# Cross-attention and an expert FFN on one core: the read-outs and scores of a quad gathered in one cluster, and the low rank of the last quad turned between two tiles

## The chip, the core and the metric

The kernel runs on one core of a Trainium2 chip. The core has TensorE for matrix products, VectorE (DVE in the profile), ScalarE (ACT), GpSimd (POOL) and SyncE (SP), which here issues the DMAs. The engines run side by side, each through its own list of instructions in order, and wait for each other by semaphores. All data is fp32.

The metric is the device time of one execution in microseconds (us). Before the change the median of three runs is 1106.21 us (1106.09 to 1106.55).

## What is computed

There are 8 batches of 1024 rows of width 1024. Each batch has 64 memory tokens of the same width and a mask over them.

```python
# reference, cut: attention over the memory, then an expert FFN, each with a residual
h      = layernorm(x)
scores = where(mask, einsum('bsd,bmd->bsm', h, mem) / sqrt(D), -1e30)
x      = x + einsum('bsm,bmd->bsd', softmax(scores), mem)
h      = layernorm(x)
base   = h @ weight.T                         # 1024 x 1024
gates  = top 2 of softmax(h @ router_w.T) over 8 experts, made to sum to 1
Ax     = einsum('nd,erd->ner', h, lora_A)     # 8 experts of rank 16
x      = x + base + 2 * einsum('ner,ne,eor->no', Ax, gates, lora_B)
```

A batch whose mask leaves no token gets no read-out.

## The kernel before

**Tiles and quads.** The 8192 rows are 64 tiles of 128 rows. Two tiles make a pair, and two pairs make a quad: pairs u and v = u + 1. After a prologue that handles the first pairs, `quad(u)` runs for u = 2, 4, ... 30. It does the FFN of u and v, and between its matmuls the attention of later pairs: n = u + 2, m = u + 3 and f = u + 4. The whole order of every engine is written out by hand (`manual_schedule`): engines take their instructions in the order in which the Python code calls them. A `hook` is a function that is called after a given step of a product or joint, so that its work is put there.

**The FFN.** The 1024 x 1024 product is done with Strassen-like block products, which need sums of blocks. Most of these sums are on POOL. A quad consists of:
- product 1 of u, then of v, into a bank called ch (128x512, line 691);
- the low rank of each pair, `rt_low_rank_tile` (line 569), two tiles of 16 matmuls of 128x136 into pa: projections on the experts and the router's logits. ACT copies pa to axl (line 574). `rt_top` on DVE then picks two experts and scales axl (lines 582 to 603). `rt_turn_low_rank` transposes axl on TensorE into trw (line 609), ACT copies it to axwt (line 611), and `lora` (line 683) multiplies it by the experts' second factors;
- six `joint` products of u and v together, numbered 6, 2, 7, 3, 5, 4, with banks jl and ju (lines 683 and 691). Each has step hooks 0 to 7. `joint_sums` prepares its operands on POOL, and DVE adds its results to the rows (line 805).

Before pa the normalised rows go through DRAM and back in blocks (`hs`), and `rt_turn_tile` transposes them on DVE into hA and hB (line 89).

**The attention of a pair.** ACT takes sums and squares of the rows (`x_sums`, `x_squares`, lines 195 and 204). The rows are loaded a second time in blocks (`xs`, eight DMAs a pair from SP, line 83) and DVE transposes them into xT (line 89). `att_scores` multiplies xT by the turned memory memT: 32 matmuls of 128x64 weights, two side by side on the halves of the array (sct, line 410). ACT copies the scores, TensorE transposes them (sc, line 424), DVE scales and shifts them (`att_shift`), ACT takes the exponential (line 446), and DVE divides (`att_divide`, lines 454 and 455). TensorE transposes the weights (ptp, line 460), and ACT copies these to pt (line 462). `att_readout` multiplies pt by the memory: 8 matmuls with 64 rows of weights, again two side by side (ro, line 471). DVE adds the result to the rows (`att_add`). `f_sums`, `f_squares`, `f_std` and `f_rows` then normalise the rows for the FFN on ACT and DVE.

**The memory of a batch.** Four pairs share one batch. In a quad with f at the first pair of a batch (`new_mem`), `load_ms` loads the memory in blocks, `turn_mem` transposes it on DVE and sums it on POOL (lines 363 to 365), and `centre_turned` has TensorE form means (line 373) that DVE subtracts (line 374).

**Where read-out and scores stand.** Each quad has two clusters. The first follows pa of u: ro n and sct m, then trw u and ch of v. The second follows pa of v: ro m and sct f, then jl of joint 6:

```python
        if more:
            att_readout(n)
            att_scores(m)
            if u > 2:
                rt_turn_low_rank(u)
        ...
        product(v, 1, low_u)
        ...
        rt_low_rank_tile(v, 0)
        if more:
            att_turn_p(m)
        rt_low_rank_tile(v, 1, (lambda: centre_turned(b)) if new_mem else None)
        ...
            att_readout(m)
        if far:
            att_scores(f)
```

**Buffers.** There are eight PSUM banks: six in ps_pp (`bank_of`: ch, ro, jl, ju, means), one in ps_at (sct, sc, ptp) and one in ps_rt (pa, trw). A ring of five SBUF tiles serves xs, xT, the rows h and hs, and ms.

Of the kernel before, what the change touches and what calls it, by code (L numbers as in the profile page):

```python
# [10 lines left out]
F32 = mybir.dt.float32  # L11
# [13 lines left out]
def kernel(  # L25
# [61 lines left out]
    def transpose_blocked(dst, src):  # L87

        nc.vector.transpose(  # L89
            dst.rearrange("p k (t i) -> p t k i", i=NB),  # L90
            src.rearrange("p t (k i) -> p t k i", i=NB),
        )

    xts, xss, mems = {}, {}, {}

    def load_xs(u: int):

        xss[u] = []
        for r in range(2):
            xs = ring.tile([P, 4, QD], F32, tag="ring", name=f"xs_{u}_{r}")  # L100
            load_blocked(xs, xf[(2 * u + r) * P : (2 * u + r + 1) * P, :])
            xss[u].append(xs)

    def load_xt(u: int):
        xts[u] = []
# [237 lines left out]
    def load_ms(b: int):  # L343

        msr = ring.tile([P, D], F32, tag="ring", name=f"ms_{b}")
        n = M // NB * QD
        ms = msr[:, :n].rearrange("p (t c) -> p t c", c=QD)
        load_blocked(ms, mem[b])
        ones = msr[:, n : n + P]
        nc.gpsimd.memset(ones, 1.0 / D)  # L350
        mcs[b] = ms, ones, msr[:, n + P : n + P + M], msr

    def turn_mem(b: int):

        mt = memp.tile([P, KD, M], F32, tag="memT", name=f"memT_{b}_True", bufs=1)
        ms, ones, of_k, msr = mcs[b]
        transpose_blocked(mt, ms)
        if b == 1:
            nc.vector.tensor_reduce(of_k, mt.rearrange("p k m -> p m k"), AX.X, ALU.add)
        else:  # L360
            by = nc.gpsimd.tensor_tensor
            s4 = msr[:, : 4 * M].rearrange("p (k m) -> p k m", m=M)
            by(s4, mt[:, :4], mt[:, 4:], ALU.add)
            by(s4[:, :2], s4[:, :2], s4[:, 2:], ALU.add)
            by(of_k, s4[:, 0], s4[:, 1], ALU.add)
        mem_ts[b, True] = mt

    def centre_turned(b: int):

        _, ones, of_k, _ = mcs.pop(b)  # L370
        mt = mem_ts[b, True]
        means = bank_of(f"means_{b}")[:, :M]
        mm(means, ones, of_k, start=True, stop=True)
        tt(mt, mt, means.unsqueeze(1).to_broadcast([P, KD, M]), ALU.subtract)
# [16 lines left out]
    def xT_tile(u: int, r: int):  # L391
        t = ring.tile([P, KD, P], F32, tag="ring", name=f"xT_{u}_{r}")
        x_ts.setdefault(u, []).append(t)
        return t

    def att_turn_pe(u: int, r: int, later: bool = False):
        t = xT_tile(u, r)
        return transpose_pe((t[:, :KH, :], t[:, KH:, :]), xts[u][r], f"x{u}_{r}", later)

    def att_turn(u: int):  # L400
        for r in range(2):
            transpose_blocked(xT_tile(u, r), xss[u][r])

    def att_scores(u: int):

        mt = mem_ts[u // PPB, u > 1]
        sct = ps_at.tile([2 * M, P], F32, tag="at", name=f"sct_{u}")
        for k in range(KD):
            for r in range(2):
                mm(  # L410
                    sct[r * M : (r + 1) * M, :], mt[:, k, :], x_ts[u][r][:, k, :],
                    start=(k == 0), stop=(k == KD - 1),
                )
        scs[u] = small.tile([2 * M, P], F32, tag="tp", name=f"scts_{u}", bufs=2)
        nc.scalar.copy(scs[u], sct)
# [39 lines left out]
        tt(s, s, rden.unsqueeze(2).to_broadcast([P, 2, M]), ALU.mult)  # L455
        ps[u] = s

    def att_turn_p(u: int):
        ptp = ps_at.tile([2 * M, P], F32, tag="at", name=f"ptp_{u}")
        nc.tensor.transpose(ptp, ps.pop(u).rearrange("p j m -> p (j m)"), ident)  # L460
        pts[u] = small.tile([2 * M, P], F32, tag="tp", name=f"pt_{u}", bufs=2)
        nc.scalar.copy(pts[u], ptp)

    def att_readout(u: int):
# [13 lines left out]
    def att_add(u: int):  # L478
        for r in range(2):
            att_add_tile(u, r)  # L480
# [121 lines left out]
            ax_e = axl[:, r, :ER].rearrange("p (e r) -> p e r", r=R)  # L602
            tt(ax_e, ax_e, we[:, r, :].unsqueeze(2).to_broadcast([P, E, R]), ALU.mult)

    def rt_turn_low_rank(u: int):
        axl = axls.pop(u)
        trw = ps_rt.tile([ER, 2, P], F32, tag="rt", name=f"trw_{u}")
        for r in range(2):
            nc.tensor.transpose(trw[:, r, :], axl[:, r, :ER], ident)  # L609
        axwts[u] = small.tile([ER, 2, P], F32, tag="axwt", name=f"axwt_{u}", bufs=2)  # L610
        nc.scalar.copy(axwts[u], trw)
# [66 lines left out]
    def add(u: int, bank, r: int, c: int):  # L678
        xc = xts[u][r][:, ts(c, HB)]
        tt(xc, bank, xc, ALU.add)  # L680
# [39 lines left out]
            for to in {1: ((0, 0),), 6: ((0, 1),), 7: ((1, 0),), 8: ((1, 1),)}[i]:  # L720
                add(u, chain, *to)

    def one_add(u: int):

        for to in ((0, 0), (0, 1), (1, 0)):
            add(u, pps[u][1], *to)

    def t_of(u: int):

# [43 lines left out]
        by(s3, up[:, :HK], lo[:, :HK], ALU.subtract)  # L773
        jss[i] = s1, s2, s3, s4

    def joint(i: int, u: int, hooks, final: bool = False):

# [13 lines left out]
        def to_x(p, src, first: int, n: int):  # L793
            if i == 6:
                t = t_of(p)[:, first : first + n]
                if n == HH and (p == u and first == 0 or v == NP - 1):
                    nc.scalar.copy(t, src)
                elif n == HH:
                    nc.vector.tensor_copy(t, src)
                else:  # L800
                    tt(t, src, t, ALU.add)  # L801
                return
            for row, col in BOTH.get(i, ((r, c),)):
                xc = xts[p][row][:, col * HB + first : col * HB + first + n]
                tt(xc, src, xc, ALU.add)  # L805
# [273 lines left out]

    def quad(u: int):  # L1080

        v, n, m, f = [u + i for i in range(1, 5)]
        more = n < NP
        far = f < NP
        b = f // PPB
        new_mem = far and f % PPB == 0

        product(u, 1, (lambda: att_sc(n)) if u == 2 else None, 1)
        if more and u > 2:
            x_sums(m)  # L1090
        if new_mem:
            mask_bias(b)
        pending.pop()()
        if u == 2:
            att_divide(n)
        one_add(u)
        rt_low_rank_tile(u, 0)
        if u == 2:
            att_turn_p(n)
        rt_low_rank_tile(u, 1)  # L1100
        if u == 2:
            att_turn(m)
        rt_turn_tile(v, 0)
        rt_top(u)
        rt_turn_tile(v, 1)
        rt_sum_3(u)
        rt_sums(v)
        if more and u > 2:
            x_squares(m)
        if new_mem:  # L1110
            load_ms(b)
        if far:
            load_xs(f)
            load_xt(f)
        if more:
            att_readout(n)
            att_scores(m)
            if u > 2:
                rt_turn_low_rank(u)
                x_root(m)  # L1120
                att_add(n)

        low_u = {3: lambda: rt_turn_low_rank(u)}
        if more:
            low_u = {0: lambda: att_sc(m), 2: lambda: product(u, 8)}
            if u == 2:
                low_u[1] = lambda: rt_turn_low_rank(u)
        product(v, 1, low_u)
        if more:
            att_rstd(m)  # L1130
            att_exp(m)
            if u == 2:
                att_add(n)
                att_divide(m)
        else:
            product(u, 8)
        product_add(u, 8)
        if more:
            f_sums(n)
            if u > 2:  # L1140
                att_divide(m)
        if new_mem:
            turn_mem(b)
        one_add(v)
        rt_low_rank_tile(v, 0)
        if more:
            att_turn_p(m)
        rt_low_rank_tile(v, 1, (lambda: centre_turned(b)) if new_mem else None)
        joint_sums(6, u)
        rt_sum_3(v)  # L1150
        if far:
            att_turn(f)
        rt_top(v)
        if more:
            f_squares(n)
            f_std(n)
            att_readout(m)
        if far:
            att_scores(f)
        if new_mem:  # L1160
            load_mem(b)
        if more:
            att_add(m)

        hooks = {7: [lambda: rt_turn_low_rank(v)]}
        if more:
            row_0, row_1 = f_rows_steps(n)
            hooks = {2: [row_0], 5: [lambda: rt_turn_low_rank(v), row_1]}
        end_6 = joint(6, u, hooks)
        joint_sums(2, u)  # L1170

        def low_v():
# [5 lines left out]
            for p in (u, v):  # L1178
                six_add(p)

        hooks = {1: [six]}
        if far:
            x_stats(f)
            hooks[3] = [lambda: att_sc(f)]
        if new_mem:
            void_mem(b)
        if (f + 2) % PPB == 0 and f + 2 < NP:
# [19 lines left out]
            hooks[5].append(lambda: att_exp(f))  # L1207
        end_3 = joint(3, u, hooks)
        joint_sums(5, u)
        if m + 2 < NP:  # L1210
            load_xs(m + 2)

        hooks = {1: [end_3]}
        if far:
# [8 lines left out]
        def rows_0():  # L1223
            end_5()
            for p in (u, v):
                store(p, 0)
                if not more:
                    store(p, 1, ts(1, HB))
            if m + 2 < NP:
                load_xt(m + 2)  # L1230

        hooks = {1: [rows_0]}
        if more:
            hooks[3] = [lambda: rt_sums(n)]
        if m + 2 < NP:
            hooks[5] = [lambda: att_turn(m + 2)]
        end_4 = joint(4, u, hooks, not more)

        def last():
# [56 lines left out]
```

## Time and profile before

| what | value |
|---|---|
| median of 3 runs | 1106.21 us |
| the profiled execution | 1106.56 us |
| its span, first to last instruction | 1104.7 us |
| instructions | 17542 |
| DMA traffic | 174.01 MB, mean 158 GB/s |
| ch (line 691), 248 matmuls 128x512 from hA | 115.8 us busy |
| pa (line 569), 1024 matmuls of 128x136 | 71.1 + 69.9 us busy |
| ro (line 471), 256 matmuls with 64 weight rows | 63.6 us busy |
| sct (line 410), 960 matmuls with 64 weight columns | 62.0 us busy |
| trw (line 609), 64 transposes | 13.3 us busy |
| sums of a tile on ACT (lines 195 and 204), mean of one | 1.05 and 1.15 us |
| xT transposes on DVE (line 89), mean of one | 1.23 us |
| xs loads (line 83), from issue to landing | 3.6 us |

The profile is one execution with the hardware's profiler on. Lines are those of the kernel before. "Busy" counts an instruction from its start to its end; matmuls overlap each other in TensorE's pipeline, so that a mean duration is longer than the distance from one start to the next. In a timeline each row gives the start, the duration of the run of equal instructions that begins there, the engine, the line and operation, out and in by the program's names, the shapes and how many there are. A bracket tells how long the engine was idle before and what released it. The 1.86 us between the span and the time of the profiled execution lie outside the program's instructions.

### The profile page before, as it was taken

Reading aid. Unit: us, or ns where it says so; the run is one execution under the profiler, and the core shown is the slowest. Engines: PE = TensorE matmul, PEld = TensorE weight load, DVE = VectorE, ACT = ScalarE, POOL = GpSimd, SP = SyncE. Lnnn points to the kernel's source line nnn. Section 1 sums busy time; section 2 is a strip of 40 time slices with the busy share of each in tenths; the row PEclk is TensorE's granted clock in tenths of the full one; section 3 lists DMA queues with packets and bytes.
Section 4 is the critical chain, followed back from the end, with each engine's and each line's share of the span. In section 5 each row is a group of like instructions: output and inputs, shape, how many; then the busy total and the mean of one; then the engine's idle time right before and its main releaser. Section 6 shows DMA issues by size and latency. Waiting matters only on the chain.

```text
span 1104.7 us, 17542 instructions
## 1 busy us (share of the span) xinstructions
PE 1095.7 (99%) x5864; PEld 848.1 (77%) x5864; DVE 810.8 (73%) x2063; ACT 555.3 (50%) x1063; POOL 575.9 (52%) x647
## 2 busy tenths in 40 slices
PE   8999999999999999999999999999999999999998
PEld 6554787887878778787887878778787887878877
DVE  6666968777786768867678686777868787686665
ACT  4577554718357282663727547173562826545010
POOL 0079564735637265473635647266372744637382
PEclk9999999999999999999999999999999999999999
DMA  9857356374554735456265553754446453532301
GB/s 230 210 177 222 113 166 201 100 238 132 154 182 136 222 109 183 151 164 218 77 211 162 154 190 101 215 166 157 153 139 203 145 190 132 158 131 91 138 1 77
DMA packets 104922, 174.01 MB, mean 158 GB/s; under 512 B 12929, under 2 KB 77441, under 8 KB 104833
## 3 DMA queue, kind: packets, MB, share of 16 engines
q1 hardware_dynamic: 104832, 172.90, 50.3%
q8 instruction: 47, 0.77, 0.3%
q14 instruction: 43, 0.34, 0.1%
HBM read 107.84 MB, written 65.01 MB: 156 GB/s over the span
## 4 chain that ended last, share of the span: by engine, by line
PE 98%; DVE 1%; ACT 0%; DMA 0%; issue 0%; SPq 0%; DVEq 0%; ACTq 0%
PE jl L691 28%; PE ju L691 21%; PE pa L569 11%; PE ch L691 10%; PE sct L410 6%; PE ro L471 5%; PE ju L683 4%; PE jl L683 3%; PE plain L691 3%; PE ch L683 2%; PE j L691 1%; PE trw L609 1%; DMA xt<-in_x_dram 0%; PE tr_x L385 0%; PE b L691 0%; PE ptp L460 0%
## 5 line engine op out<-in xcount | busy, mean ns | idle before, releaser
L805 DVE TENSOR_TENSOR xt<-jl,xt 128x256 f32<-128x256 f32 x421 | 191.3, 484 | 115.8 <-PE jl L691 75.6
L805 DVE TENSOR_TENSOR xt<-ju,xt 128x256 f32<-128x256 f32 (+1 forms) x210 | 110.6, 550 | 69.9 <-PE ju L691 67.3
L623 POOL TENSOR_TENSOR s<-hA,hB 128x512 f32<-128x512 f32 x31 | 39.6, 1278 | 208.8 <-PE jl L691 92.8
L195 ACT ACTIVATE junk<-xt 128x1024 uint8<-128x1024 f32 x60 | 63.2, 1053 | 138.2 <-DMA xt<-in_x_dram 137.7
L735 POOL TENSOR_TENSOR xt<-xt,hA 128x512 f32<-128x512 f32 x90 | 111.3, 1275 | 23.5 <-DVE hA L801 23.4
L691 PE MATMUL ch<-w,hA 128*128 128x512 f32 x248 | 115.8, 593 | 0.0
L630 POOL TENSOR_TENSOR hA<-hA 128x512 f32<-128x512 f32 x31 | 39.4, 1272 | 141.3 <-PE pa L569 141.3
L691 PE MATMUL ju<-w,s_j 128*128 128x256 f32 x360 | 94.3, 384 | 0.2
L691 PE MATMUL ju<-t,s_j 128*128 128x256 f32 x360 | 92.5, 379 | 0.0
L680 DVE TENSOR_TENSOR xt<-ch,xt 128x512 f32<-128x512 f32 x124 | 79.4, 680 | 8.4 <-PE ch L691 4.5
L680 DVE TENSOR_TENSOR xt<-ro,xt 128x512 f32<-128x512 f32 x128 | 79.2, 676 | 3.3 <-PE ro L471 3.3
L691 PEld LDWEIGHTS ju<-t,s_j 128*128 128x128 f32 x360 | 66.2, 190 | 16.3 <-issue 3.6
L691 PEld LDWEIGHTS ch<-w,hA 128*128 128x128 f32 x248 | 44.6, 190 | 42.7 <-issue 41.8
L691 PEld LDWEIGHTS ju<-w,s_j 128*128 128x128 f32 x360 | 63.9, 190 | 16.4 <-issue 7.4
L691 PE MATMUL jl<-t,s 128*128 128x256 f32 x300 | 76.0, 384 | 0.0
L569 PEld LDWEIGHTS pa<-art_sb,hA 128*128 128x128 f32 x512 | 66.3, 190 | 9.0 <-issue 5.0
L89 DVE STREAM_TRANSPOSE xT<-xs 128x1024 f32<-128x1024 f32 x60 | 72.6, 1228 | 0.5
L410 PEld LDWEIGHTS sct<-xT,memT_True 128*64 128x64 f32 x960 | 53.1, 137 | 24.8 <-issue 12.1
L569 PE MATMUL pa<-art_sb,hB 128*128 128x136 f32 x512 | 71.1, 280 | 0.0
L569 PE MATMUL pa<-art_sb,hA 128*128 128x136 f32 x512 | 69.9, 279 | 0.0
L204 ACT ACTIVATE junk<-xt,of_x 128x1024 uint8<-128x1024 f32 x60 | 68.7, 1145 | 1.5
L253 ACT ACTIVATE junk<-xt,of_f 128x1024 uint8<-128x1024 f32 x60 | 68.7, 1145 | 1.5
(205 smaller groups left out, 2448.6 us busy)
## 6 DMA issues: line engine op xcount, KB each, us to landing
xt<-in_x_dram SPq DMA_DIRECT2D x64, 512.0 KB, 4.6
out_dram<-xt SPq DMA_DIRECT2D x62, 512.0 KB, 2.7
xs<-in_x_dram SPq DMA_DIRECT2D x240, 128.0 KB, 3.6
hd<-h SPq DMA_DIRECT2D x60, 512.0 KB, 2.7
hs<-hd SPq DMA_DIRECT2D x240, 128.0 KB, 3.2
mem<-in_ctx_dram SPq DMA_DIRECT2D x16, 256.0 KB, 3.8
w<-in_w_t_dram SPq DMA_DIRECT2D x16, 256.0 KB, 10.2
ms<-in_ctx_dram SPq DMA_DIRECT2D x28, 64.0 KB, 2.5
```

What stands on the lines that cost most here:

```text
L89: nc.vector.transpose(dst.rearrange("p k (t i) -> p t k i", i=NB), src.rearrange("p t (k i) -> p t k i", i=NB),)
L195: nc.scalar.activation(nowhere, xts[u][r], AF.Identity, accum_out=sm[:, r, :])
L204: nc.scalar.activation(nowhere, xts[u][r], AF.Square, bias=nm[:, r, :], accum_out=ss[:, r, :],)
L253: nc.scalar.activation(nowhere, xts[u][r], AF.Square, bias=nm[:, r, :], accum_out=ss[:, r, :])
L410: mm(sct[r * M : (r + 1) * M, :], mt[:, k, :], x_ts[u][r][:, k, :], start=(k == 0), stop=(k == KD - 1),)
L471: mm(ro, pts[u][rows, :], m[rows, ts(c, HB)], start=True, stop=True)
L569: mm(pa[:, r, :], h, art_sb[:, k, :], start=(k == 0), stop=(k == KD - 1))
L680: tt(xc, bank, xc, ALU.add)
L683: mm(bank, axwts[u][:, r, :], lb_sb[:, c0 : c0 + n], start=alone, stop=True, skip_group_check=True)
L691: mm(bank, a[:, k, :], w[:, k, :], start=(start and k == 0), stop=(k == n - 1), skip_group_check=True)
L735: nc.gpsimd.tensor_tensor(xc, xc, t_of(u), ALU.add)
L805: tt(xc, src, xc, ALU.add)
```

## The change

The diff moves the attention one pair further ahead, with a new name g = u + 5.

- **One cluster.** In the quads u = 4 to 26 both clusters are replaced by one behind pa of v: ro n, sct f, sct g, ro m, then jl of joint 6. The scores of m are already there from the quad before; `att_scores(g, True)` writes to a bank of ps_pp, and `sc m` is transposed in ch of v. All four transposes xT of f and g stand ahead of the cluster on DVE. The quad u = 2 has two clusters (ro n, sct m and sct f, sct g, ro m), u = 28 has ro n between the tiles of pa v, and ro m ahead of joint 6.
- **The low rank of u.** trw u moves from the cluster to between the two tiles of pa v, with a bank of its own from ps_pp. In the last quad, u = 30, it moves there from behind ch of v, and `product(u, 8)` (the low rank into ch u) follows pa of v.
- **Loads.** `load_xs` takes single tiles. In joint 4 SP issues, behind the stores of the first tiles, both tiles of xt g, both xs of f + 2 and the first of g + 2; the second xs of g and xt f come early in the next quad.
- **Memory.** load_ms, turn_mem and centre_turned of the next batch move to the quad before the one with its first pair f: behind sct g, in joint 6 (hook 5) and in joint 2 (hook 5). The sums are one `tensor_reduce` on DVE in place of three additions on POOL.
- **Smaller moves.** x_squares m follows x_sums m directly, both ahead of pa u's copy on ACT. `one_add(v)` is split, its last part in joint 6. `f_squares`, `f_std` and `f_rows` of n go to joints 6 and 2. pt m is written over s m.

```diff
     def turn_mem(b: int):
...
-        if b == 1:
-            nc.vector.tensor_reduce(of_k, mt.rearrange("p k m -> p m k"), AX.X, ALU.add)
-        else:
-            by = nc.gpsimd.tensor_tensor
-            s4 = msr[:, : 4 * M].rearrange("p (k m) -> p k m", m=M)
-            by(s4, mt[:, :4], mt[:, 4:], ALU.add)
-            by(s4[:, :2], s4[:, :2], s4[:, 2:], ALU.add)
-            by(of_k, s4[:, 0], s4[:, 1], ALU.add)
+        nc.vector.tensor_reduce(of_k, mt.rearrange("p k m -> p m k"), AX.X, ALU.add)
...
-    def att_scores(u: int):
+    def att_scores(u: int, apart: bool = False):
...
+        if apart:
+            sct = bank_of(f"sct_{u}")[:, :P]
+        else:
+            sct = ps_at.tile([2 * M, P], F32, tag="at", name=f"sct_{u}")
...
     def quad(u: int):
...
-        if more and u > 2:
+        if late:
             x_sums(m)
+            x_squares(m)
...
         rt_turn_tile(v, 0)
         rt_top(u)
+        if late:
+            x_root(m)
+            product(v, 1, lambda: att_sc(m))
+            att_rstd(m)
+            att_shift(m)
+            att_exp(m)
         rt_turn_tile(v, 1)
+        if late and far:
+            att_turn_tile(f, 0)
+            load_xs(g, (1,))
         rt_sum_3(u)
         rt_sums(v)
...
+        if late:
+            att_divide(m)
+            if far:
+                att_turn_tile(f, 1)
+            rt_low_rank_tile(v, 0)
+            rt_turn_low_rank(u, bank_of(f"trw_{u}")[:, : 2 * P])
+            one_add(v, (0,))
...
         else:
+            product(v, 1)
+            rt_low_rank_tile(v, 0)
+            rt_turn_low_rank(u, bank_of(f"trw_{u}")[:, : 2 * P])
+        if far:
+            for r in range(2):
+                att_turn_tile(g, r)
+        if late and not far:
+            att_readout(n)
+            att_add(n)
+        rt_low_rank_tile(v, 1)
+        if late:
+            att_turn_p(m, True)
+        if not early:
             product(u, 8)
-        product_add(u, 8)
...
         joint_sums(6, u)
         rt_sum_3(v)
+        if late and far:
+            att_readout(n)
+        product_add(u, 8)
+        if late and far:
+            att_add(n)
         if far:
             att_scores(f)
+            att_scores(g, True)
...
+        if far or not more:
+            rt_top(v)
+        if more:
+            att_readout(m)
...
         hooks = {1: [six]}
         if far:
             x_stats(f)
             hooks[3] = [lambda: att_sc(f)]
+        if more:
+            hooks[3].append(lambda: f_rows(n))
+        if next_mem:
+            hooks[5].append(lambda: centre_turned((f + 2) // PPB))
...
-            if m + 2 < NP:
-                load_xt(m + 2)
+            if far:
+                load_xt(g)
+            if f + 2 < NP:
+                load_xs(f + 2)
+                load_xs(g + 2, (0,))
```

## The prediction

> **What bounds the kernel now.** I read the shares first, then the chain of waits, because a busy share alone does not say what sets the end.
>
> ```profile
> PE 1095.7 (99%) x5864; PEld 848.1 (77%) x5864; DVE 810.8 (73%) x2063; ACT 555.3 (50%) x1063; POOL 575.9 (52%) x647
> ...
> PE 98%; DVE 1%; ACT 0%; DMA 0%; issue 0%; SPq 0%; DVEq 0%; ACTq 0%
> ```
>
> TensorE is busy 99% and carries 98% of the chain; the clock row is 9s throughout. So time is saved only where TensorE issues fewer matmuls or issues the same ones more densely. The change keeps the matmuls, so I look for density: start-to-start steps in TensorE's timeline, taken from undisturbed stretches and from both clusters of a quad.
>
> ```profile
> 514.59 1.09 PE L569 MATMUL pa<-art_sb,hB 128*128 128x136 f32 x8
> 515.61 1.99 PE L471 MATMUL ro<-mem,pt 64*128 64x512 f32 x8
> 517.53 1.97 PE L410 MATMUL sct<-xT,memT_True 128*64 128x128 f32 x32
> 519.42 0.44 PE L609 MATMUL trw<-ident,axl 128*128 128x128 f32 x2
> 519.70 1.02 PE L691 MATMUL ch<-w,hA 128*128 128x512 f32 x2
> ...
> 524.11 1.09 PE L569 MATMUL pa<-art_sb,hA 128*128 128x136 f32 x8
> 525.03 1.09 PE L569 MATMUL pa<-art_sb,hB 128*128 128x136 f32 x8
> ...
> 529.93 1.97 PE L410 MATMUL sct<-xT,memT_True 128*64 128x128 f32 x32
> 531.83 1.99 PE L691 MATMUL jl<-t,s 128*128 128x256 f32 x8
> ...
> 596.72 2.42 PE L410 MATMUL sct<-xT,memT_True 128*64 128x128 f32 x32
> 599.07 1.99 PE L691 MATMUL jl<-t,s 128*128 128x256 f32 x8
> ```
>
> The first number is the start. Eight pa take 525.03 - 524.11 = 0.92, a step of 0.116. A pair of ro steps 0.429 (as every 128x512 does), a pair of sct 0.109, a trw 0.109. So from 514.59 to 519.70 dense issue would need 8 x 0.116 + 4 x 0.429 + 16 x 0.109 + 2 x 0.109 = 4.61 us; it took 5.11. The **0.50** too much sits where the tile shape changes (128x128, 64x128, 128x64), in single starts: pa to ro 0.197 over, ro to sct 0.147, sct to trw 0.156. The second cluster (to jl) loses 0.548, its last step being 0.204. Both: 1.047 per quad. The last two pairs show a second loss: sct to jl is 1.90 in one quad and 2.35 in the next. That is 0.456 in each of the six quads that begin a new batch of memory, and there the row of the waits and DVE's timeline name it:
>
> ```profile
> PEld sct L410 <- DVE xT L89: 8.1, 15, 0.8
> ```
> ```profile
> 594.16 0.69 DVE L374 TENSOR_TENSOR memT_True<-memT_True,means 128x512 f32<-128x512 f32 x1 [0.55 <-PE means L373]
> 594.76 2.36 DVE L89 STREAM_TRANSPOSE xT<-xs 128x1024 f32<-128x1024 f32 x2
> ```
>
> The scores start at 596.72 while DVE is still turning their second tile (to 597.1), because turning and centring the memory (memT, means) stood ahead.
>
> **The twelve quads u = 4 to 26.** *Switches.* One cluster ro n, sct f, sct g, ro m has four changes: pa to ro 0.197, ro to sct 0.147, sct to ro, ro to jl 0.202 (a cluster of ro alone loses 0.399 in all, less 0.197). Sct to ro is not in the trace: at least 0.147 (ro to sct), at most 0.204 (sct to full); I take 0.20, since both ends leave the sct shape for a 64- or 128-row one. Sum 0.746, gain 0.30 x 12 = **3.6** (0.05 x 12 more at the low end).
>
> *New memory.* In six quads turn_mem and centre_turned leave the cluster's approach for joints 6 and 2 of the quad before, and the sums go from POOL to DVE. DVE's xT then no longer waits for them: 6 x 0.456 = **2.74**. After these clusters the first jl steps lose a further 0.06 to 0.075, which should go too: 6 x 0.07 = 0.4. In the joints DVE has room: about 0.7 for the transpose (128x512), an estimated 0.7 for the reduce (same 512 columns), 0.69 for the centring, once in two quads, where it idles 0.27 of the time.
>
> *The order that must hold.* With t = 0 at the first ch of u and the steps above, TensorE runs pa u 3.87 to 7.57, ch v from 7.57, sc m 8.43, pa v tile 0 at 11.11, trw u 12.97, tile 1 13.19, ptp m 15.04, ch u's low rank 15.15, ro n 16.10, sct f 18.02, sct g 19.82, ro m 21.67, jl of joint 6 23.59. What each wait finds, with durations of before's rows in the new order:
> - trw u (12.97) needs rt_top of u, which ends 10.76 on DVE. It now sits in a bank of its own, so that pa and trw do not exchange one. The ch low rank behind it (15.15) waits for ACT's axwt copy, 0.37 after 13.2: covered by 1.5.
> - ptp m (15.04) needs the divided s. DVE: shift and reduce to 11.72, both transposes of v's second tile to 13.01, xT f 0 to 14.09, reciprocal, divide at 14.29, done 14.5. Cover 0.45. Behind a late ptp stand both ch's low rank and the cluster.
> - sct g waits for its xs. These four DMAs wait on SP for the slot that hB v 1 leaves (13.01); four such loads landed 4.15 to 4.2 us after their first issue (582.29 to 586.49), so 17.2, just when xT g 1 can start (17.42). It ends 18.6; cover 1.2. Sct g also takes the bank of ch u, read by product_add to 19.23 (cover 0.5).
> - jl and ju of joint 6 want banks that the ro n adds (done 21.5) and the first ro m add (24.7) free: cover 0.65 at ju (25.42).
> - ptp and pt in place save nothing and cost nothing: one ACT copy either way. The split one_add and the later f_rows are beside PE; joint 2's low rank wants axwt v, cover 0.45.
>
> *ACT and SP.* x_sums m and x_squares m (1.17 and 1.26 a tile) now both precede ACT's axl copy (7.77), so the second xt m must land by 3.87 (0.45 late costs nothing yet). Before it was there by 2.05 to 3.23, in two quads at 4.2. In joint 4 six xs transfers (0.43 to 0.48 issue each on SP) now queue directly behind it, in place of loads that came later; below nothing is excluded, since the xt itself is issued no earlier. Between 0 and 0.5 late; I take 0.3, which passes the tolerance in few quads: **-0.4** in all.
>
> **The three other quads.** u = 28 keeps two clusters, both of ro alone (before 0.50 with sct, and 0.40). The first moves between pa's tiles; about 0.15 of switches goes, but its sct is now done in the quad before and joint 6 comes too early for DVE and ACT: a new wait, estimated 0.45 from the same rows laid in order. **-0.3**. u = 2 keeps two clusters, with one change of shape more (0.2) and sct 7 waiting about 0.55 for its xs; the 0.57 by which its second cluster exceeds 0.55 goes: **-0.2**. In the last quad:
>
> ```profile
> 1052.92 1.12 PE L683 MATMUL ch<-lb_sb,axwt 128*128 128x512 f32 x2 [0.46 <-ACT axwt L611]
> ```
> ```profile
> 1060.27 1.30 POOL L630 TENSOR_TENSOR hA<-hA 128x512 f32<-128x512 f32 x1
> ```
> ```profile
> 1061.60 0.37 ACT L797 COPY hA<-ju 128x256 f32<-128x256 f32 x1 [1.65 <-POOL hA L630]
> 1062.02 1.13 PE L691 MATMUL ju<-t,s_j 128*128 128x256 f32 x4
> ```
>
> Trw and the wait for axwt (0.154 + 0.655) go behind pa. But POOL's chain does not move: hA is released at 1061.57, ACT copies, and the matmul at 1062.02 is already 0.10 late for it. So the 0.81 is given back there. Only later, where trw of v at 1063.86 waited 0.256 and its neighbour 0.056 for DVE's rt_top, is **+0.3** left, because that starts earlier.
>
> **Sum.** 3.6 + 2.74 + 0.4 - 0.4 - 0.3 - 0.2 + 0.3 = 6.2. The profiled execution took 1106.56 (span 1104.7 and 1.86 around it): 1100.4. The median shown, 1106.21, is 0.35 lower; I say **1100.2**.
>
> **A rule against the change.** The new place of the divide is under POOL's rt_sums of v. A 128x128 divide with both inputs in SBUF is in the trace on both sides:
>
> ```profile
> 524.00 0.73 POOL L770 TENSOR_TENSOR s_j<-s 128x256 f32<-128x256 f32 x1
> ```
> ```profile
> 524.37 0.50 DVE L455 TENSOR_TENSOR s<-s,of_s 128x128 f32<-128x128 f32 x1
> ...
> 590.92 0.29 DVE L455 TENSOR_TENSOR s<-s,of_s 128x128 f32<-128x128 f32 x1
> ```
>
> Under POOL it ended only after POOL's end (524.73), 0.21 longer than with POOL idle. The Trainium skill (SBUF — State Buffer, Who interferes with whom) makes it a rule: a DVE instruction with two SBUF inputs contends with a GpSimd one that reads SBUF, and the loser is blocked for the whole instruction. Here POOL's instructions are not 0.73 but 1.27 us. By the 0.21 row ptp keeps 0.25 of cover. By the rule it depends on which one: POOL's first sum runs 13.09 to 14.36, the next from 14.44. A divide at 14.29 slips into the gap and ends 14.5; one more than 0.15 later is blocked to 15.71. I take the gap, as both sides count from the same event, the end of hB v 1.
>
> **Rivals.**
> - *The gap is missed* (slower). s ends 15.85, ptp waits 0.81, in 12 quads 9.7: about **1110**. For it: 0.15 of room. Against: the spacings on both engines repeat.
> - *The second xt is late by 1 us or more.* axl u, rt_top u and the low rank behind it slide, about 0.55 x 12 = 6.6, which eats the gain: **1106.6**. For it: two quads at 4.2 already. Against: SP's order keeps xt ahead of the xs.
> - *A part fails*: xs g lands 1.5 late, so that sct g waits 0.3 x 12, or switching shapes costs as much in one cluster as in two and only the memory's stalls go: **1103.5**.
>
> **Chances.** Forecast 0.56 (alone 1098.6 to 1102.4), a part failing 0.13, xt late 0.14, gap missed 0.17. A change under 0.2% (2.2 us) can't be told from none here: faster is below 1104.0, slower above 1108.4. So faster 0.69, same 0.14, slower 0.17. The range 1098.6 to 1107.0 leaves out the gap missed and little more.
>
> **What would show it.** Right: in the quads pa to jl with about 0.75 over dense steps, ptp at its step behind pa, quads of new memory as long as the others, the ju at the last quad's joint 6 waiting near 0.9. Wrong: an idle before ptp with a divide over 1 us; axl copies later than 0.2 after pa; sct g preceded by a wait on xT or on ch.

## The result and the profile after

The changed kernel took **1108.33 us** (median of 20 runs, 1105.28 to 1112.11), the kernel before 1106.12 (20 runs, 1105.73 to 1106.86). The ratio is 1.002, with a 95% interval of 1.0012 to 1.0028. So it is slower by about 2 us where 6 us less were forecast, and what is new besides is the spread: 6.8 us between runs, where it was 1.1. The profiled execution is one of the long ones: 1111.43, 3.1 above the median, with a span of 1109.7.

The page of the kernel after, parts 1 and 4:

```profile
PE 1092.1 (98%) x5864; PEld 846.1 (76%) x5864; DVE 815.8 (74%) x2069; ACT 557.3 (50%) x1063; POOL 567.1 (51%) x629
...
PE 80%; DMA 8%; DVE 6%; ACT 3%; SPq 1%; issue 1%; POOL 1%; DVEq 0%; ACTq 0%
```

TensorE is busy 3.6 us less in a span 5.0 us longer, and the chain that ended last, 98% TensorE before, now runs through DMA for 8% and through DVE and ACT for 9%. Some quads wait for transfers. First a quad that doesn't, TensorE's timeline (the first number is the start):

```profile
190.55 1.02 PE L691 MATMUL ch<-lb_sb,axwt 128*128 128x512 f32 x2
191.51 1.99 PE L476 MATMUL ro<-mem,pt 64*128 64x512 f32 x8
193.42 3.71 PE L411 MATMUL sct<-xT,memT_True 128*64 128x128 f32 x64
197.07 1.99 PE L476 MATMUL ro<-mem,s 64*128 64x512 f32 x8
198.99 1.35 PE L699 MATMUL jl<-t,s 128*128 128x256 f32 x5
```

This is the one cluster. From the last ch ahead of it to the second jl it loses 0.75 us over the dense steps of the prediction, which was the sum forecast (0.746). From the first sct to the second ro it takes 197.07 - 193.42 = 3.65 for 32 pairs, of which the change from sct to ro is 0.20 over the dense step. Such a quad is 66.26 us long from ch to ch, or 66.48 where means are formed in it; before it was 66.56, or 67.31 with new memory. Twelve quads without a wait are 796.2, against 803.2 before: 7.0 gained. But they took 806.4 in this execution, because of two kinds of wait, 10.1 us in all. The first is ahead of the second tile of pa v. In the quad that begins at 578.90:

```profile
591.88 0.38 PE L617 MATMUL trw<-ident,axl 128*128 128x128 f32 x2
593.34 1.19 PE L574 MATMUL pa<-art_sb,hA 128*128 128x136 f32 x8 [1.08 <-DVE hA L89]
...
595.52 0.30 PE L462 MATMUL ptp<-ident,s 128*128 128x128 f32 x1
```

Two trw need 0.22; here the next start is 1.46 later. DVE's hA v 1 was late, since rt_top u ahead of it waited for axl. DVE's timeline shows that wait, and ACT's what was behind it:

```profile
589.06 0.24 DVE L587 MAX8 top<-axl 128x8 f32<-128x8 f32 x2 [2.40 <-ACT axl L579]
```
```profile
584.83 1.06 ACT L194 ACTIVATE junk<-xt 128x1024 uint8<-128x1024 f32 x1 [4.25 <-DMA xt<-in_x_dram]
...
586.24 1.15 ACT L203 ACTIVATE junk<-xt,of_x 128x1024 uint8<-128x1024 f32 x1
...
587.52 1.15 ACT L203 ACTIVATE junk<-xt,of_x 128x1024 uint8<-128x1024 f32 x1
588.66 0.36 ACT L579 COPY axl<-pa 128x272 f32<-128x272 f32 x1
```

The second xt of m lands at 584.74, 5.84 after the quad's start. One sum and two squares later ACT copies axl, 9.76 after the start and not 7.77, as in a quad without a wait. Six quads lose 6.85 us in this way. The rows of SP's issues show what stands behind that xt (SP's timeline, then the DMA view of a window that holds the second xt's issue alone: KB each, us from issue to landing):

```profile
575.88 1.48 SPq L107 DMA_DIRECT2D xt<-in_x_dram  x2
577.48 9.59 SPq L83 DMA_DIRECT2D xs<-in_x_dram  x12
587.17 0.85 SPq L874 DMA_DIRECT2D out_dram<-xt  x2
```
```profile
xt<-in_x_dram SPq DMA_DIRECT2D x1, 512.0 KB, 7.7
```

The second wait is inside the cluster (TensorE, then DVE, in the quad that begins at 308.30):

```profile
326.32 1.97 PE L411 MATMUL sct<-xT,memT_True 128*64 128x128 f32 x32
329.82 1.97 PE L411 MATMUL sct<-xT,memT_True 128*64 128x128 f32 x32 [1.53 <-DVE xt L688]
```
```profile
327.95 1.25 DVE L89 STREAM_TRANSPOSE xT<-xs 128x1024 f32<-128x1024 f32 x1 [1.99 <-DMA xs<-in_x_dram]
329.12 0.65 DVE L688 TENSOR_TENSOR xt<-ch,xt 128x512 f32<-128x512 f32 x1
```

DVE waits 1.99 for the second xs of g, and product_add of ch u, whose bank sct g takes, is queued behind that transpose. The releaser named for sct g is this add; the cause is the DMA one step further back. Four quads lose 3.3 us here. Both figures belong to this long execution. In one of median length the two waits together cost about 7 us and not 10.1 (an estimate: 10.1 less the 3.1 between the two, if nothing else differs).

### The profile page after: what moved, and what is told of

Same layout as the page of the kernel before. It is cut to its first block, busy times and chain, and to the rows that moved or that the text cites. A ratio compares the mean times of both kernels' runs of the same rounds, so it can differ in the third digit from the quotient of the medians.

```text
span 1109.7 us, 17564 instructions
## 1 busy us (share of the span) xinstructions
PE 1092.1 (98%) x5864; PEld 846.1 (76%) x5864; DVE 815.8 (74%) x2069; ACT 557.3 (50%) x1063; POOL 567.1 (51%) x629
## 4 chain that ended last, share of the span: by engine, by line
PE 80%; DMA 8%; DVE 6%; ACT 3%; SPq 1%; issue 1%; POOL 1%; DVEq 0%; ACTq 0%
PE jl L699 26%; PE ju L699 20%; PE pa L574 6%; PE ro L476 5%; PE ch L699 5%; PE sct L411 5%; DMA xt<-in_x_dram 4%; PE ju L691 3%; PE jl L691 3%; PE plain L699 3%; PE ch L691 2%; DMA out_dram<-xt 2%; DVE xt L814 2%; ACT junk L203 2%; DMA xs<-in_x_dram 1%; PE j L699 1%
## 5 line engine op out<-in xcount | busy, mean ns | idle before, releaser
L295 ACT ACTIVATE h<-xt,of_f 128x1024 f32<-128x1024 f32 x60 | 71.2, 1232 | 23.1 <-DVE of_f L291 17.2
```

Source lines behind the costliest of these rows:

```text
L295: nc.scalar.activation(h, xts[u][r], AF.Identity, bias=nmr[:, r, :], scale=rstd[:, r, :])
```

## The experiments

Each ratio is to the kernel before, run beside it on the same chip. Its medians there were 1106.66 (beside the xs behind the stores, the four left there, the xt of f ahead, and both edits), 1106.25 (beside the two with loads from ACT and the last quad) and 1106.38 (beside the whole rows and ACT's order). What is said of single quads is read from one profiled execution of each.

**The xs loads behind the stores.** In place of right behind xt m in joint 4:

```diff
             if far:
                 load_xt(g)
-            if f + 2 < NP:
-                load_xs(f + 2)
-                load_xs(g + 2, (0,))
...
         def last():
             end_4()
             if more:
                 for p in (u, v):
                     store(p, 1)
+            if f + 2 < NP:
+                load_xs(f + 2)
+                load_xs(g + 2, (0,))
```

> The changed kernel, but in each quad the twelve xs loads that SP issues behind the second xt of m go behind the last two stores of the quad instead (some 4 us later). Theory A (the second xt shares the DMA engines with the xs loads issued right behind it and lands late): the second xt lands by 4.2 us after the quad's start in every quad, as before the change, in place of up to 5.9; ACT copies axl at 7.77; no wait stands between trw u and the second tile of pa v (six waits of 0.27 to 1.25 us in the profile of the changed kernel); about 4 to 5 us come off the median, 1103.5 to 1104.5, and the runs spread less. The waits before sct g (3.3 us) stay. Theory B (it is the sum of the traffic, or DRAM, that is slower, whatever the order): the second xt lands as late as now and the time stays at 1107.5 to 1109. Theory C (the xs are now late in turn): a wait of xT f on the xs before the cluster, 1106 or more.

Measured: **1103.14** (6 runs, 1101.88 to 1104.69), ratio 0.9968 [0.9956, 0.998]. The second xt of m lands between 2.24 and 3.27 in all twelve quads, axl is copied at 7.77 in each, and no wait is left at pa v. Before sct g two waits are left (1.31 and 0.70). That these fell too, from 3.3 to 2.0, was not expected, and the median is a little below the range. SP's order (the sixteen are the twelve and then the second xs of g) and the landing of that xt in this kernel:

```profile
572.55 1.47 SPq L107 DMA_DIRECT2D xt<-in_x_dram  x2
576.82 3.88 SPq L874 DMA_DIRECT2D out_dram<-xt  x2
580.80 9.55 SPq L83 DMA_DIRECT2D xs<-in_x_dram  x16
```
```profile
xt<-in_x_dram SPq DMA_DIRECT2D x1, 512.0 KB, 4.9
```

These are the same bytes in another order: theory A holds. B is refuted by the landing, C by the absence of a wait of xT f.

**Four of the twelve left there.**

```diff
             if f + 2 < NP:
-                load_xs(f + 2)
-                load_xs(g + 2, (0,))
+                load_xs(f + 2, (0,))
...
+            if f + 2 < NP:
+                load_xs(f + 2, (1,))
+                load_xs(g + 2, (0,))
```

> As the first of these runs, but four of the twelve xs loads (512 KB) stay right behind the second xt of m. Theory A: the delay grows with what is issued behind: the second xt lands between, up to about 5.0 us after the quad's start, few or no waits at pa v, 1103.5 to 1106. Theory B: as the changed kernel, 1107.5 to 1109.

Measured: 1105.76 (13 runs, 1103.24 to 1108.35), ratio 0.9996 [0.9988, 1.0004]. The second xt lands between 2.10 and 5.01. With part of the loads behind it part of the delay is there, and the spread comes back with it (5.1 us between runs, 2.8 with none left there).

**The same bytes as whole rows.** With True, `load_xs` issues one DMA of 512 KB for a tile in place of four. For these three tiles this kernel leaves out the blocking that the scores need; the work of every engine stays.

```diff
-                load_xs(f + 2)
-                load_xs(g + 2, (0,))
+                load_xs(f + 2, (0, 1), True)
+                load_xs(g + 2, (0,), True)
```

> The changed kernel, but the three xs tiles that SP loads right behind the second xt of m in joint 4 are loaded as whole rows (three DMAs of 512 KB with rows of 4 KB, in place of twelve of 128 KB with pieces of 1 KB): the same bytes in the same place, all issued within 1.5 us. The blocks of these tiles are then not those that the scores need, so the attention's output is not the reference's. If it is the bytes behind it that make the second xt late, its landing is as late as now, up to 5.9 us after the quad's start, and the waits at pa v stay: 1106 to 1110. If it is the short pieces, the second xt lands by 4.2 us in every quad, the waits at pa v go: 1102 to 1104.5.

Measured: 1104.12 (7 runs, 1102.51 to 1105.74), ratio 0.9979 [0.9967, 0.999]. The second xt lands by 3.67 in ten quads, and at 4.57 and 4.64 in two. Most of the delay goes with the short pieces (or the number of DMAs, which changes with them); in two quads a part remains with the bytes alone. Neither theory holds by itself.

**Both xt of f ahead of the second xs of g.**

```diff
             att_turn_tile(f, 0)
+            load_xt(f)
             load_xs(g, (1,))
...
-        elif far:
-            load_xt(f)
```

> The changed kernel, but SP issues both xt of f ahead of the four loads of the second xs of g, not behind them. If xs g lands late because the xt are behind it in the queue, then its last DMA lands within 3 us of its issue in every quad (now up to 4.8), the waits before sct g (3.3 us over four quads in the profile) go, and the waits at pa v stay: 1105 to 1107. If the four DMAs are late because they wait for the slot of hB v 1 alone, nothing changes: 1107.5 to 1109. If the xt, now in flight ahead, delay xs g more: above 1109.

Measured: **1132.4** (5 runs), ratio 1.0232 [1.0218, 1.0246]: a miss in size, but the third outcome. These xt wait on SP for a slot that the last stores leave, and then go out about 2 us ahead of the xs. In one quad (SP's timeline, and the DMA view of the four xs):

```profile
533.40 1.55 SPq L107 DMA_DIRECT2D xt<-in_x_dram  x2
535.82 1.75 SPq L83 DMA_DIRECT2D xs<-in_x_dram  x4
```
```profile
xs<-in_x_dram SPq DMA_DIRECT2D x4, 128.0 KB, 4.3
```

With two xt in flight ahead of them, the xs take 4.3 us in this quad, and 5.0 (median) in all twelve against 2.6 in the changed kernel. Every quad now waits before sct g. The second xt of m comes past 4.3 in eleven quads and not six; no run shows why.

**Both edits.**

> The changed kernel with both edits of SP's order. If both waits come from transfers queued behind, neither is left in the twelve quads, each of which takes 66.25 us, or 66.48 with means: 796.4 for the twelve, and with what the other quads take in the profile of the changed kernel 1101.5 in all, range 1100.5 to 1103, spread as small as before the change. If the order only moves the collision, 1105 or more.

Measured: **1151.96** (5 runs, 1149.12 to 1156.98), ratio 1.041 [1.0391, 1.0429]. The order only moved the collision, and worse than thought. With the xs later, both xt of f queue behind twelve xs and still ahead of the second xs of g. DVE's row of waits, and sct g on TensorE in one quad:

```profile
DVE xT L89 <- DMA xs<-in_x_dram: 46.4, 12, 5.4
```
```profile
552.95 3.36 PE L411 MATMUL sct<-xT,memT_True 128*64 128x128 f32 x32 [3.89 <-DVE xt L688]
556.24 1.99 PE L476 MATMUL ro<-mem,s 64*128 64x512 f32 x8
```

A long wait can cost twice. From this sct g to ro it is 556.24 - 552.95 = 3.29 us, where a quad without a wait has 1.85: the granted clock from 552.37 to 556.50 was 0.59. The waits before sct g are 38.2 of the 56.1 us that the twelve quads lose, and the mean granted clock of this execution is 0.985 (1.0 with the first edit alone), which is some 17 of its 1155 us (an estimate: 0.015 of them).

**The xt of f from ACT, late.** ACT issues them behind its copy of sct f, when the second xs of g has landed. With the first edit, and alone:

```diff
             att_scores(f)
+            if late:
+                load_xt(f, nc.scalar)
             att_scores(g, True)
```

> The kernel with the xs loads behind the stores, and in addition the two xt of f are issued by ACT behind its copy of sct f (some 20 us after the quad's start) and not by SP right behind the second xs of g. If the two waits before sct g that were left there (1.31 and 0.70 us) come from the xt right behind, they go, the twelve quads take 66.25 or 66.48 us each, and the median is 1101.0 to 1102.0, spread within 1 us. If they come from something else, or ACT's issue holds up its copies, 1103 or more.

Measured: **1102.09** (5 runs, 1101.94 to 1102.44), ratio 0.9963 [0.995, 0.9977]. The chain is TensorE's again, the spread is gone, and in eleven of the twelve quads the steps run on without a wait:

```profile
PE 93%; DVE 2%; DMA 2%; SPq 1%; POOL 1%; issue 0%; ACT 0%; DVEq 0%; ACTq 0%
```
```profile
587.22 0.38 PE L617 MATMUL trw<-ident,axl 128*128 128x128 f32 x2
587.44 1.09 PE L574 MATMUL pa<-art_sb,hA 128*128 128x136 f32 x8
...
589.29 0.27 PE L462 MATMUL ptp<-ident,s 128*128 128x128 f32 x1
...
592.28 3.71 PE L411 MATMUL sct<-xT,memT_True 128*64 128x128 f32 x64
```

One wait of 0.40 before sct g is left, in the quad u = 8, and the median is just above the range expected. This version is faster than both kernels.

> The changed kernel with this second edit alone: the xs loads stay right behind the second xt of m, the xt of f are issued by ACT. Theory A (two separate collisions): the waits before sct g go, those at pa v stay: 1105.5 to 1107.5, with a spread of several us. If the late xt of m alone makes the quads late and xs g only follows it, no change: 1107.5 to 1109.

Measured: 1104.23 (10 runs, 1102.13 to 1108.63), ratio 0.9985 [0.9975, 0.9996]: better than expected. Two waits before sct g (0.97 and 0.69) and, in five quads, waits of up to 0.9 at pa v and ptp remain in its profile; the second xt of m lands past 4.3 in five quads, at 5.15 at the latest. That the waits at pa v shrink too, from 6.85 to about 1.9, was not foreseen, and its cause stays open. So the two collisions are not separate: in these profiles each edit by itself lessens both waits.

**ACT's order.** Is it the late xt, or that x_squares m now stands ahead of the axl copy?

```diff
             x_sums(m)
-            x_squares(m)
...
+            x_squares(m)
             x_root(m)
```

> The changed kernel, but ACT takes x_squares m behind its copy of axl u and the exponential of rt_top, not ahead of the copy. The order on ACT is then no longer what makes a late xt m count: axl is copied at 7.77 even where the xt lands at 5.9. But the root, and with it s m, comes 2.5 us of squares later: DVE waits for it ahead of hA v 1, so that pa v's second tile waits about 1.4 us and ptp a little more in every quad: 15 to 25 us in all, 1118 to 1126. If ACT has the room, the waits at pa v go and the time is 1103 to 1105.

Measured: 1130.36 (one run). ACT in one quad, and TensorE there:

```profile
594.93 0.39 ACT L579 COPY axl<-pa 128x272 f32<-128x272 f32 x1 [1.01 <-PE pa L574]
```
```profile
601.80 1.19 PE L574 MATMUL pa<-art_sb,hA 128*128 128x136 f32 x8 [1.29 <-DVE hA L89]
```

axl is on time in all twelve quads, though the xt lands at up to 5.46. But each quad pays 1.46 at pa v and 0.36 behind it, 21.8 in all, and u = 28 another 4.4, which was not in the expectation. So the two conditions are tied: the squares must come early for s m, and then the xt must be early for axl.

**The last quad as before**, on the kernel with the xs behind the stores:

```diff
-            product(v, 1)
-            rt_low_rank_tile(v, 0)
-            rt_turn_low_rank(u, bank_of(f"trw_{u}")[:, : 2 * P])
+            product(v, 1, {3: lambda: rt_turn_low_rank(u)})
+            product(u, 8)
+            product_add(u, 8)
+            rt_low_rank_tile(v, 0)
```

> The kernel with the xs loads behind the stores, and in the last quad the low rank back at its old place: trw u behind ch v, then ch u's low rank, then pa v. If the 0.81 us is given back at joint 6 as predicted, the wait there falls from 1.06 to about 0.1 to 0.3 us, and from the last quad's first ch to the end it takes 0.2 to 0.4 us more than with the change (63.6 us). If the turn itself was worth its 0.81, it takes 0.8 more.

Measured (one run): from the last quad's first ch to the end of the span 63.96, against 63.52 with the change in the kernel it was made from. The rows of this run, and of the changed kernel:

```profile
1048.99 1.12 PE L691 MATMUL ch<-lb_sb,axwt 128*128 128x512 f32 x2 [0.46 <-ACT axwt L619]
...
1057.12 1.03 PE L699 MATMUL jl<-t,s_j 128*128 128x256 f32 x4
1058.09 1.13 PE L699 MATMUL ju<-t,s_j 128*128 128x256 f32 x4
```
```profile
1065.37 1.03 PE L699 MATMUL jl<-t,s_j 128*128 128x256 f32 x4
1067.30 1.13 PE L699 MATMUL ju<-t,s_j 128*128 128x256 f32 x4 [0.90 <-ACT hA L806]
```

With the change the wait for axwt goes, and the one at joint 6 (jl to ju, over four steps of 0.216) grows from 0.11 to 1.06. Of the 0.81, 0.30 (the changed kernel against the one before) to 0.44 (this pair) is kept.

## Why the prediction was wrong

As printed, its terms add to 6.14 and not 6.2, and 6.2 below the median of 1106.21 is 1100.0 and not 1100.2; neither slip matters. Term by term, by the profiles:

- **Switches, new memory and the jl behind it** (6.7): right. Twelve quads without a wait gain 7.0, the cluster loses 0.75 as worked out, and sct to ro costs 0.20, as taken.
- **The second xt of m** (-0.4): the step that failed. "Between 0 and 0.5 late; I take 0.3, which passes the tolerance in few quads." It was up to 1.7 later than its latest landing before (5.84 against 4.13), passed the tolerance of about 4.3 in six quads, and cost 6.85 us. The mechanism was named, and the rival was given one chance in seven. That its price, 6.6, is close to 6.85 is luck: 6.6 was twelve quads at 0.55, and the 6.85 are six quads at 0.62 to 1.61. The reason set against it, that SP's order keeps the xt ahead of the xs, was no reason: the xt did land ahead of them in every quad, but late.
- **The second xs of g**: "cover 1.2" was computed from four loads that had landed 4.15 to 4.2 after their first issue. Now, with two xt issued behind them, the last landed up to 6.1 after it, and they cost 3.3 us. These two terms, 10.1 together in this execution, turn the gain of 7.0 into a loss. They were held as separate rivals and never added, so the range ended at 1107.0.
- **The gap for the divide**: right. In the quad that begins at 308.30 POOL's first sum ends at 322.93 and the next starts at 323.01:

```profile
321.65 1.27 POOL L631 TENSOR_TENSOR s<-hA,hB 128x512 f32<-128x512 f32 x1 [5.19 <-DVE hB L89]
323.01 1.28 POOL L632 TENSOR_TENSOR s<-s,hA 128x512 f32<-128x512 f32 x1
```
```profile
322.78 0.30 DVE L456 TENSOR_TENSOR s<-s,of_s 128x128 f32<-128x128 f32 x1
```

  The divide starts under the first sum and ends at 323.08. In all twelve quads it takes 0.29 or 0.30, as long as with POOL idle, and ends 0.14 to 0.15 behind the sum, as it did before the change (524.87 behind 524.73). Whether the sum held it up for its first half, as the rule cited has it, these rows can't tell. The slower case on record did not occur; ptp is late only in quads where hA v 1 already was.
- **u = 28** (-0.3): mis-sized. One sct (1.74) left this quad, yet it is only 0.39 shorter. So 1.35 was given back, where 0.3 was forecast (a new wait of 0.45 less 0.15 of switches). It was given back at joint 6, where jl and ju wait for ACT and DVE:

```profile
1006.29 1.10 PE L699 MATMUL jl<-t,s_j 128*128 128x256 f32 x4 [0.68 <-ACT hA L806]
...
1008.11 1.13 PE L699 MATMUL ju<-t,s_j 128*128 128x256 f32 x4 [0.49 <-DVE hA L808]
```

- **u = 2** (-0.2): -0.8, mis-sized too. The ch of u = 4 starts 2.53 later; 1.74 of it is that sct, now done here, the rest the wait for xT g 1 (0.59), the extra switch and the means. **u = 30** (+0.3): +0.30.

Without the two waits the sum of the measured terms is 7.0 - 0.8 - 1.35 + 0.30 = 5.15, which makes 1101.4 of the profiled 1106.56; the version with both loads out of the way took 1102.09 (median). The forecast was a good account of TensorE's steps and a bad one of the DMA queue.

## What to carry to other kernels

When a change packs an engine more densely, write down for each transfer when it must have landed, and judge it by what is issued behind it as well as ahead: its measured landing belongs to the traffic around it and does not move with it. A spread of several us between runs, where there was one of about 1, pointed here to a transfer at the edge of its cover. And rivals that can happen in the same quad are added before the range is set.

## What the runs showed of the hardware

A DMA is delayed by DMAs that the same engine issues after it, although all of them land in the order of issue. Landing of the second xt of m (512 KB), us after the quad's start, twelve quads of one profile each (from about 4.3 on TensorE has to wait):

| issued right behind it | earliest | latest | past 4.3 |
|---|---|---|---|
| before: the stores, 3.7 us later | 1.97 | 4.13 | 0 |
| changed: 12 DMAs of 128 KB in pieces of 1 KB | 2.16 | 5.84 | 6 |
| 4 such DMAs | 2.10 | 5.01 | 3 |
| 3 DMAs of 512 KB in rows of 4 KB | 2.73 | 4.64 | 2 |
| the stores, then the 12 (first edit) | 2.24 | 3.27 | 0 |

One profile is one execution. That of the changed kernel is a long one (1111.43, median 1108.33), and that with four DMAs is the shortest of its thirteen (1103.24, median 1105.76). The medians over all runs give the same order: 1103.14 with the first edit, 1104.12 with rows of 4 KB, 1105.76 with four, 1108.33 with twelve. Of the twelve, SP issues only seven before the xt has landed, in each of the twelve quads: 0.9 MB in pieces of 1 KB delay it more than 1.5 MB in rows of 4 KB.

The trace of the changed kernel shows where the delay sits. It records sixteen steps of each DMA's semaphore, one for each part of the transfer. In the quad that begins at 578.90, eleven parts of the xt are in 1.78 after the quad's start and the last at 5.84. Of the xs issued next, thirteen parts are in by 3.41. So most of the transfer is as early as in a good quad, and the landing is that of the slowest part. The Trainium skill (DMA: Bandwidth & Descriptors, Queues, rings and completion order) says that each DMA engine takes its descriptors in ring order, and that completion is nonetheless not first in, first out. In these profiles all DMAs of SP (744 in the changed kernel) land in the order of issue, and being first in that order did not keep the xt on time.

Why the same order gives 2.2 in one quad and 5.8 in the next stays open. In all six late flights of the changed kernel there is an instruction fetch (queue q8 of the DMA view, one packet of 16 KB, 0.9 to 1.7 us; in one flight only near its end), in the other six there is one. In the flight from 577.02 to 584.74:

```profile
q8 instruction: 1, 0.02, 0.8%
```

With the first edit seven flights have such a fetch and none lands past 3.27, so it does not make the xt late by itself, and no run leaves it out.
